# A selective scan's input products, two channel groups at a time, into a pair of PSUM banks of their own

## The chip, the cores and the metric

The kernel runs on one core of one Trainium2 chip. The metric is the device time of one execution in microseconds, the median of several runs. The profile is one further execution, recorded by the hardware profiler. The engines are called as the profile calls them: PE (matmul), PEld (its weight loads), DVE (the vector engine), ACT (the scalar engine, also called ScalarE), POOL (GpSimd) and SP, which here only issues DMAs.

## The reference, cut to what matters

A MetaFormer layer on four images of 256 channels and 32 x 32 points (1024 points), all in float32: a Mamba-like selective scan in four blocks of 64 channels, gated convolutions, attention with 8 heads, a depthwise convolution and projection, and then a mixture of 8 experts of which each point uses 2. The change is about the scan:

```python
def selective_scan(u, dt, Bm, Cm, A, Dp):          # u, dt: (B, 1024, 128); Bm, Cm: (B, 1024, 16); A: (128, 16)
    dA = jnp.exp(dt[..., None] * A)
    dBu = (dt * u)[..., None] * Bm[:, :, None, :]

    def step(h, inp):
        dA_t, dBu_t, C_t = inp
        h = dA_t * h + dBu_t
        return (h, jnp.einsum('bds,bs->bd', h, C_t))
    ...                                              # scan over the 1024 points
    return ys.transpose(1, 0, 2) + u * Dp
```

For each of 4 images and 4 blocks there are thus 128 channels x 16 states, each a recurrence over 1024 points. The products `dBu` are what the change touches.

## The kernel before, in words

**The scan.** The 1024 points are cut in two halves of 512, so there are 4 x 4 x 2 = 32 parts `(b, n, h)`. The 128 x 16 recurrences of a part do not fit the 128 partitions at once: they are done in `NSTEP` = 16 steps of 128 rows, where step `i = 4q + g` holds channel group `g` (32 channels) under four states of group `q`. Each step makes:

- `decay` (L718, ACT): `dA = exp(dt * A)`, three steps ahead (`LEAD` = 3);
- `inflow` (L728, DVE): `dBu = (dt * u) * B`, a 128x512 product, written to PSUM;
- `step` (L739, DVE): the recurrence itself, one scan operation over 512 points, which reads `dA` from SBUF and `dBu` from PSUM and writes `hs`; then (L747, POOL) `hs * C`, written over `dA`. In the first half the last column is kept by a small ACT copy (L745), and the second half starts from it;
- `sums_of` (L757, PE): adds the four states of each channel by a matmul with `quads`, into the bank `yp` of the part.

The inputs have to be laid out so that all four state rows carry the same channels. `spread_dt` (L681) copies one channel group of `dt` and `dt * u` by four DMAs on SP from the part's tile `dt` into a tile `dts` with 4 KB a partition; there are six such tiles (pool `steps4`). `spread_c` (L704) does the same for `C` from DRAM, and `spread_b` (L710) makes the rows of `B` by matmuls into a PSUM bank `bs`, one for each `q`.

**PSUM.** There are eight banks of 128 x 512 floats, all in one pool under one tag. Every matmul result draws one, and so does `dBu`, except that for `g` = 3 the product is written over `bs`, which is not read again afterwards. A bank is given out when all that used it has been done; the framework places the semaphore waits, between two operations of the same engine as well.

**The order.** All engines run the program in the order written. `scan(at, i, stop)` issues what belongs to one step: matmuls and DMAs for the next part by the tables `before`, `behind` and `group`, then `decay` for step i+3, then `inflow` for step i+1, then `step` for i. Background work (normalisations, convolutions, products around attention) consists of generators, and after each step `beat()` lets each of them issue a piece. For images 1 to 3 the scan stops in the middle of the image (`stop`), the attention of the image before runs with only light work beside it, and `resume` takes the scan up again when the last steps of attention have been issued.

**Attention.** `attention(b)` has 32 steps `(g, h, kt)`: `logits` makes four `st` banks by matmul (L1126), ACT takes their exponentials (L1136), and PE adds up values (L1175) and sums (L1147) in two further banks `av`, which live for the eight `kt` of a block and are read by `end_block` (L1159, L1163) in the second step of the next block.

**Experts.** After the scan PE works through tiles of 256 or 320 points (`Experts.tile`): a hidden layer (L2332, banks `h`), then the output `y` (L2365) into a bank of its own, which DVE reads with the bias (L2383, or L2374 and L2375 for a last block of 64 points). From the second tile on, the weights lie in the tiles of the scan's step sizes: three of `dts` and one of `dt` for each tile of points, so that two tiles' weights are there at a time.

Of the kernel before, what the change touches and what calls it, by code (L numbers as in the profile page):

```python
# [9 lines left out]
F32 = mybir.dt.float32  # L10
AF = mybir.ActivationFunctionType
ALU = mybir.AluOpType
AX = mybir.AxisListType

P = 128
C = 256
NC2 = C // P
HH = WW = 32
N = HH * WW
HALF = 512  # L20
NB, DM, DIN, DS, DTR, KC = 4, 64, 128, 16, 4, 4
NHEAD, HD = 8, 32
NE, DFF = 8, 1024
NHC = DFF // P
# [10 lines left out]
_AT = {}  # L35
# [43 lines left out]
def network(  # L79
# [27 lines left out]
    nc = tc.nc  # L107
    shifted = sums is None
    B = x.shape[0]

    cpool = ctx.enter_context(tc.tile_pool(name="consts", bufs=1))
    psum = ctx.enter_context(tc.tile_pool(name="psum", bufs=8, space=bass.MemoryType.PSUM))

    def ps_tile(name):

# [10 lines left out]
    def col(name, i=0, rows=slice(0, P)):  # L126
# [3 lines left out]
    ident = cpool.tile([P, P], F32, name="ident")  # L130
# [5 lines left out]
    eps5 = cpool.tile([P, 1], F32, name="eps5")  # L136
# [6 lines left out]
    nc.gpsimd.memset(one, 1.0)  # L143

    experts = Experts(
        ctx, tc, psum, B, vecs[:, _AT["b1"] : _AT["b1"] + NE * NHC], ident, eps5, ones_mean, Wg, bg,
        W1, W2, b2, out,
    )

# [1 line left out]
    with tc.tile_pool(name="w_conv", bufs=1) as wp, tc.tile_pool(  # L151
# [1 line left out]
    ) as act8, tc.tile_pool(name="act4", bufs=8) as act4, tc.tile_pool(  # L153
        name="act2", bufs=16
    ) as act2, tc.tile_pool(name="steps", bufs=2) as actd, tc.tile_pool(
        name="steps4", bufs=6
    ) as acts, tc.tile_pool(name="rows", bufs=3) as actc, tc.tile_pool(
        name="small", bufs=1
    ) as small, tc.tile_pool(
# [227 lines left out]
        def ps(name):  # L387

            return psum.tile([P, HALF], F32, tag="ps", name=name)
# [284 lines left out]
            )  # L674

        def spread_dt(b, n, h, g):
            t = T[b, n, h, "dts", g] = acts.tile(
                [P, 2, HALF], F32, tag="dts", name=f"dts_{b}_{n}_{h}_{g}"
            )
            for r in states:  # L680
                nc.sync.dma_start(t[r], T[b, n, h, "dt"][ts(g, 32)])  # L681

        def project_c(b, n):
            cp = T[b, n, "cp"] = ps(f"cp_{b}_{n}")
# [30 lines left out]
        def decay(b, n, h, i):  # L715
            q, g = divmod(i, GD)
            dA = T[b, n, h, "dA", i] = a2(f"dA_{b}_{n}_{h}_{i}")
            nc.scalar.activation(  # L718
                dA, T[b, n, h, "dts", g][:, 0, :], AF.Exp, scale=A[:, g, n, q : q + 1]
            )  # L720

        ends = []

        def inflow(b, n, h, i):
            q, g = divmod(i, GD)
            dBu = T[b, n, h, "bs", q] if g == GD - 1 else ps(f"dBu_{b}_{n}_{h}_{i}")
            T[b, n, h, "dBu", i] = dBu
            nc.vector.tensor_tensor(  # L728
                dBu, T[b, n, h, "dts", g][:, 1, :], T[b, n, h, "bs", q], ALU.mult
            )  # L730

        def step(b, n, h, i):
            q, g = divmod(i, GD)
            dBu = T.pop((b, n, h, "dBu", i))
            hs = a2(f"hs_{b}_{n}_{h}_{i}")
            if h == 0 and i == 0:
                T[b, n, "last"] = small.tile([P, NSTEP], F32, tag="last", name=f"last_{b}_{n}", bufs=2)
            last = T[b, n, "last"][:, i : i + 1]
            nc.vector.tensor_tensor_scan(  # L739
                hs, T[b, n, h, "dA", i], dBu, 0.0 if h == 0 else last, ALU.mult, ALU.add  # L740
            )
            if h == 0:
                ends.append((last, hs[:, HALF - 1 : HALF]))
            if ends and (h == 1 or len(ends) > 2):
                nc.scalar.copy(*ends.pop(0))  # L745
            dA = T[b, n, h, "dA", i]
            nc.gpsimd.tensor_tensor(dA, hs, T[b, n, h, "cs", q], ALU.mult)  # L747
# [92 lines left out]
        def scan(at, i, stop):  # L840

            b, n, h = parts[at]
            q, g = divmod(i, GD)
            if g == 1 and q + 1 < GS:
                spread_b(b, n, h, q + 1)
            if at > 0:
                for what, *args in before.get(i, ()):
                    if parts[at - 1] not in finished:
                        what(*parts[at - 1], *args)
            if at + 1 < len(parts):  # L850
                for what, *args in behind.get(i, ()):
                    if what is not spread_b or not stop:
                        what(*parts[at + 1], *args)
            nb, nn = (b, n + 1) if n + 1 < NB else (b + 1, 0)
            if nb < B:
                for what, *args in group[h].get(i, ()):
                    what(nb, nn, *args)
            if g == 0 and q + 1 < GS:
                spread_c(b, n, h, q + 1)
            if g == 1 and q > 0:  # L860
                sums_of(b, n, h, q - 1)
            ahead = i + LEAD
            if ahead < NSTEP:
                decay(b, n, h, ahead)
            elif at + 1 < len(parts) and not stop:
                decay(*parts[at + 1], ahead - NSTEP)
            if i + 1 < NSTEP:
                inflow(b, n, h, i + 1)
            elif at + 1 < len(parts) and not stop:
                inflow(*parts[at + 1], 0)  # L870
            step(b, n, h, i)

        finished = set()

# [232 lines left out]
        def attention(b):  # L1107
# [12 lines left out]
            def logits(g, h, kt):  # L1120

                q, k = qk[g][:, 0, :], qk[g][:, 1, :]
                sts = [ps(f"st_{b}_{g}_{h}_{kt}_{i}") for i in range(4)]
                for i in range(4):
                    r = ts(i, HD)
                    nc.tensor.matmul(  # L1126
                        sts[i], k[r, ts(kt, P)], q[r, half(h)], start=True, stop=not shifted
                    )
                    if shifted:
                        nc.tensor.matmul(  # L1130
                            sts[i], ones[HD * i : HD * i + 1, :],
                            rows[g][HD * i : HD * i + 1, half(h)], start=False, stop=True,
                        )
                es = [a2(f"e_{b}_{g}_{h}_{kt}_{i}") for i in range(4)]
                for i in range(4):
                    ins = nc.scalar.activation(es[i], sts[i], AF.Exp, scale=1.0 / HD**0.5)  # L1136
                T["exps"] = ins if b == B - 1 else None
                return es
# [26 lines left out]
            for at, (g, h, kt) in enumerate(steps):  # L1165
                es = ahead
                if pairs and (kt % 2 or at > len(steps) - 6):
                    sum_pair()
                if at + 1 < len(steps):
                    ahead = logits(*steps[at + 1])  # L1170
                if kt == 0:

                    accs = [ps(f"av_{b}_{g}_{h}_{w}") for w in range(2)]
                for i in range(4):
                    nc.tensor.matmul(  # L1175
                        accs[0][ts(i, HD)], v8[:, kt, ts(4 * g + i, HD)], es[i],
                        start=(kt == 0), stop=(kt == NK - 1),
                    )
                if kt % 2 == 0:
                    first = es  # L1180
                else:
                    for i in range(4):
                        nc.vector.tensor_tensor(first[i], first[i], es[i], ALU.add)  # L1183
                    pairs.append((kt, accs[1], first))
                    if ending:
                        end_block(*ending.pop())
                if kt == NK - 1:
                    ending.append((g, h, *accs))
                if at == len(steps) - 3:
                    T["attended", b] = True  # L1190
                yield 1
# [204 lines left out]
        def tiles():  # L1396
# [34 lines left out]
            def load(n):  # L1431
                s, i = order[n]
                if n == 0:
                    w1 = [a8("w1_0")[:, :, 0:DFF]]
                    w2 = [a8("w2_0").rearrange("p c (k x) -> p (c k) x", x=C)]
                else:
                    w = [
                        acts.tile([P, N], F32, tag="dts", name=f"w_{n}_{k}") for k in range(3)
                    ] + [actd.tile([P, N], F32, tag="dt", name=f"w_{n}_3")]
                    w1, w2 = w[0:2], [v.rearrange("p (k c) -> p k c", c=C) for v in w[2:4]]  # L1440
                b2_s = actc.tile([P, C], F32, tag="cs", name=f"b2_{n}") if n else a2("b2_0")[:, 0:C]
                got[n] = experts.load(s, i, tables[s], w1, w2, b2_s)

# [195 lines left out]
class Experts:  # L1639
# [16 lines left out]
    ROW = C + 4  # L1656
    XR = [P, NT, ROW]

    def __init__(self, ctx, tc, psum, B, b1, ident, eps5, ones_mean, Wg, bg, W1, W2, b2, out):
        nc = self.nc = tc.nc  # L1660
        self.tc, self.psum, self.b1, self.ident, self.eps5 = tc, psum, b1, ident, eps5
        self.W1, self.W2, self.b2, self.out = W1, W2, b2, out
        self.B = B
        T, NT = self.T, self.NT
# [653 lines left out]
    def tile(self, j, s, got, hs, ys, apart=False):  # L2318
# [39 lines left out]
            added.append(ins)  # L2358

        for t, n in blocks:  # L2360
            if t % 2 == 0 or apart:
                yp = psum.tile([P, HALF], F32, tag="ps", name=f"y_{j}_{t}")
            parts = P // n
            for k in range(NHC):
                nc.tensor.matmul(  # L2365
# [154 lines left out]
```

## Time and profile before

| | |
|---|---|
| median of 3 runs | 2168.41 us (2166.26 to 2169.15) |
| the profiled execution | 2167.03 us, its span 2165.3 us |
| PE busy | 1931.0 us (89% of the span) |
| DVE busy | 1540.5 us (71%), 2252 instructions |
| ACT busy | 1212.3 us (56%) |
| POOL busy | 1043.4 us (48%) |

The span falls into the scan with its three interruptions (52 to 1438 us) and the rest, in which PE works on the last image's attention and the experts. The page's slices (each 54 us; a digit is the busy share in tenths) show it:

```
PE   6778778999977999988779999669999989999996
DVE  4989999957998989698899888987265354321121
```

DVE stands at 8 or 9 in most of the first 26 slices and low in the last 13; PE is the other way round. How to read the other views: a group's line has the line of the program, engine, operation, output and inputs, count, busy time in us, the mean of one in ns, and behind the second bar the time that the engine stood idle ahead of such an operation, with what ended it. A line of the timeline has the start and the duration in us. A line of the waits says who waited for whom: us in total, how often, and the longest.

### The profile page before, as it was taken

The numbers are of one execution on the slowest core, as the hardware profiler recorded it, in microseconds if no ns is written. First come the engines' busy times: TensorE is split into PE (matmuls) and PEld (weight loads), VectorE is DVE, ScalarE is ACT, GpSimd is POOL, SyncE is SP. The second block draws the span as 40 slices with busy tenths as digits, with TensorE's granted clock in tenths as the row PEclk, the third lists the DMA queues.
The fourth block names the chain that finished last, engine by engine and source line by source line (L and its number), as shares of the span: only waits on it lengthen the run. The fifth ranks groups of instructions, "written<-read, shape, count | busy, mean of one in ns | idle before, by whom it ended". The sixth has DMA issues, their size and how long they took to land. (4 is left out here: it accounts for less than half of the span.)

```text
span 2165.3 us, 28187 instructions
## 1 busy us (share of the span) xinstructions
PE 1931.0 (89%) x8690; PEld 867.6 (40%) x8690; DVE 1540.5 (71%) x2252; ACT 1212.3 (56%) x2272; POOL 1043.4 (48%) x931
## 2 busy tenths in 40 slices
PE   6778778999977999988779999669999989999996
PEld 2113112322211332223123223216652668888885
DVE  4989999957998989698899888987265354321121
ACT  4665657668777677776466876615268423222221
POOL 0887887812787850476877016662021012522131
PEclk8888999999999999998999999989999999999998
DMA  3555544401444431153634203444230165777764
GB/s 105 148 157 130 124 118 103 101 28 57 103 116 117 104 75 40 25 141 92 176 87 105 83 6 94 109 164 135 84 99 23 47 198 161 242 229 188 213 184 131
DMA packets 157087, 251.40 MB, mean 116 GB/s; under 512 B 34740, under 2 KB 101332, under 8 KB 156664
## 3 DMA queue, kind: packets, MB, share of 16 engines
q1 hardware_dynamic: 136560, 223.47, 37.3%
q0 software_dynamic: 12720, 17.32, 4.1%
q10 hardware_dynamic: 7640, 8.65, 1.2%
q8 instruction: 72, 1.18, 0.2%
q14 instruction: 95, 0.78, 0.1%
HBM read 137.22 MB, written 36.62 MB: 80 GB/s over the span
## 5 line engine op out<-in xcount | busy, mean ns | idle before, releaser
L747 POOL TENSOR_TENSOR dA<-hs,cs 128x512 f32<-128x512 f32 x512 | 681.1, 1339 | 376.9 <-DVE hs L739 249.8
L718 ACT ACTIVATE dA<-dts,A 128x512 f32<-128x512 f32 x512 | 359.0, 718 | 161.4 <-DMA dts<-dt 76.9
L757 PE MATMUL yp<-dA,quads 128*32 128x512 f32 x1024 | 286.3, 640 | 89.3 <-POOL dA L747 76.6
L2350 POOL DMA_INDIRECT Y<-ys,dest x68 | 109.6, 1612 | 424.3 <-DVE ys L2343 417.3
L1136 ACT ACTIVATE e<-st 128x512 f32<-128x512 f32 x512 | 263.7, 606 | 89.4 <-PE st L1126 89.2
L2337 ACT ACTIVATE hs<-h,b 128x256 f32<-128x256 f32 (+1 forms) x256 | 110.6, 478 | 343.6 <-PE h L2332 256.7
L728 DVE TENSOR_TENSOR dBu<-dts,bs 128x512 f32<-128x512 f32 x384 | 259.6, 677 | 46.0 <-PE bs L710 10.8
L739 DVE TENSOR_TENSOR_SCAN hs<-dA,last,dBu 128x512 f32<-128x512 f32 x192 | 243.6, 1269 | 3.0 <-issue 2.1
L2365 PE MATMUL y<-w,hs 128*128 128x256 f32 (+1 forms) x1088 | 242.4, 382 | 0.0
L2332 PE MATMUL h<-xT,w 128*128 128x256 f32 (+1 forms) x1024 | 239.7, 390 | 0.8 <-DVE xT L2295 0.8
L739 DVE TENSOR_TENSOR_SCAN hs<-dA,dBu 128x512 f32<-128x512 f32 x192 | 231.6, 1206 | 0.7 <-PE var L438 0.7
L1183 DVE TENSOR_TENSOR e<-e,e 128x512 f32<-128x512 f32 x256 | 168.2, 718 | 77.8 <-ACT e L1136 47.8
L2332 PEld LDWEIGHTS h<-xT,w 128*128 128x128 f32 x1024 | 195.2, 192 | 41.7 <-issue 8.0
L2365 PEld LDWEIGHTS y<-w,hs 128*128 128x128 f32 (+1 forms) x1088 | 197.3, 188 | 36.1 <-issue 9.0
L2295 DVE COPY xT<-xp 128x512 f32<-128x512 f32 (+1 forms) x36 | 23.3, 646 | 249.4 <-PE xp L2291 249.1
L710 PE MATMUL bs<-u,xpwT_s 128*32 128x512 f32 x1024 | 162.9, 669 | 40.3 <-DVE hs L739 17.3
L1126 PE MATMUL st<-qk 32*128 32x512 f32 x1024 | 174.0, 638 | 0.3
L757 PEld LDWEIGHTS yp<-dA,quads 128*32 128x32 f32 x1024 | 51.3, 114 | 303.4 <-POOL dA L747 198.7
L1175 PE MATMUL av<-e,v 128*32 128x512 f32 x1024 | 139.5, 604 | 0.0
L1953 POOL DMA_INDIRECT XS<-XR,to x64 | 65.4, 1022 | 92.0 <-ACT e L1136 53.9
L1126 PEld LDWEIGHTS st<-qk 32*128 32x128 f32 x1024 | 59.5, 183 | 115.3 <-issue 85.6
L1147 PE MATMUL av<-e,every 128*32 128x512 f32 x512 | 85.2, 596 | 2.7 <-DVE e L1183 2.6
(357 smaller groups left out, 2640.5 us busy)
## 6 DMA issues: line engine op xcount, KB each, us to landing
dts<-dt SPq DMA_DIRECT2D x512, 128.0 KB
w<-in_W_dram SPq DMA_DIRECT2D x124, 512.0 KB
cs<-cd SPq DMA_DIRECT2D x512, 64.0 KB
xs<-XS SPq DMA_DIRECT2D x32, 260.0 KB
xd<-xn SPq DMA_DIRECT2D x64, 128.0 KB
xn<-in_x_dram SPq DMA_DIRECT2D x8, 512.0 KB
XL<-xl SPq DMA_DIRECT2D x8, 512.0 KB
xl<-XL SPq DMA_DIRECT2D x4, 1024.0 KB
```

Of the source, the lines that this page charges most:

```text
L710: nc.tensor.matmul(bs[r], xpwT_s[:, n, s : s + 1].to_broadcast([P, 32]), T[b, n, "u"][:, half(h)], start=True, stop=True,)
L718: nc.scalar.activation(dA, T[b, n, h, "dts", g][:, 0, :], AF.Exp, scale=A[:, g, n, q : q + 1])
L728: nc.vector.tensor_tensor(dBu, T[b, n, h, "dts", g][:, 1, :], T[b, n, h, "bs", q], ALU.mult)
L739: nc.vector.tensor_tensor_scan(hs, T[b, n, h, "dA", i], dBu, 0.0 if h == 0 else last, ALU.mult, ALU.add)
L747: nc.gpsimd.tensor_tensor(dA, hs, T[b, n, h, "cs", q], ALU.mult)
L757: nc.tensor.matmul(T[b, n, h, "yp"][ts(g, 32)], quads, T[b, n, h, "dA", q * GD + g], start=False, stop=(q == GS - 1),)
L1126: nc.tensor.matmul(sts[i], k[r, ts(kt, P)], q[r, half(h)], start=True, stop=not shifted)
L1136: ins = nc.scalar.activation(es[i], sts[i], AF.Exp, scale=1.0 / HD**0.5)
L1175: nc.tensor.matmul(accs[0][ts(i, HD)], v8[:, kt, ts(4 * g + i, HD)], es[i], start=(kt == 0), stop=(kt == NK - 1),)
L1183: nc.vector.tensor_tensor(first[i], first[i], es[i], ALU.add)
L2332: nc.tensor.matmul(hp[:, i, :], w1(c, k0 + i), xT[:, c, :], start=(c == 0), stop=(c == NC2 - 1))
L2365: nc.tensor.matmul(yp[ts(k % parts, n), ts(t % 2, C)], hidden(k)[:, ds(t * P, n)], w2(k), start=(k < parts), stop=(k >= NHC - parts),)
```

## The change

`inflow` is done for two channel groups in one operation. A pool `psum_wide` of one tile with two neighbouring banks is added, and the common pool has six banks. `dBu` of two steps is one 128 x 2 x 512 operation into that pair, with `bs` repeated by a zero stride; the case `g` = 3 that wrote over `bs` is gone. The step sizes of two groups lie in one tile of 8 KB a partition, three tiles in place of six, and the DMAs are the same in number and size. In `scan` the product comes after `step`, at odd steps only, since there is one pair and the odd step's scan reads its second half. Outside the scan the pair of banks is used too: in attention with h = 0 for the two accumulators, with h = 1 for two of the four logits of some steps; in the experts for `y`. The experts' weights take the new tiles: one or two pairs by turns, with two `dt` tiles in the even ones.

```diff
-    psum = ctx.enter_context(tc.tile_pool(name="psum", bufs=8, space=bass.MemoryType.PSUM))
+    psum = ctx.enter_context(tc.tile_pool(name="psum", bufs=6, space=bass.MemoryType.PSUM))
+    wide_psum = ctx.enter_context(
+        tc.tile_pool(name="psum_wide", bufs=1, space=bass.MemoryType.PSUM)
+    )
+
+    def two_banks(name):
+
+        t = wide_psum.tile([P, 2, HALF], F32, tag="two", name=name)
+        return t
...
-        name="steps4", bufs=6
+        name="steps4", bufs=3
...
         def spread_dt(b, n, h, g):
-            t = T[b, n, h, "dts", g] = acts.tile(
-                [P, 2, HALF], F32, tag="dts", name=f"dts_{b}_{n}_{h}_{g}"
-            )
+            k, at = divmod(g, 2)
+            if at == 0:
+                T[b, n, h, "dts", k] = acts.tile(
+                    [P, 2, 2, HALF], F32, tag="dts", name=f"dts_{b}_{n}_{h}_{k}"
+                )
+            t = T[b, n, h, "dts", k]
             for r in states:
-                nc.sync.dma_start(t[r], T[b, n, h, "dt"][ts(g, 32)])
+                nc.sync.dma_start(t[r, at], T[b, n, h, "dt"][ts(g, 32)])
...
         def inflow(b, n, h, i):
             q, g = divmod(i, GD)
-            dBu = T[b, n, h, "bs", q] if g == GD - 1 else ps(f"dBu_{b}_{n}_{h}_{i}")
-            T[b, n, h, "dBu", i] = dBu
+            dBu = two_banks(f"dBu_{b}_{n}_{h}_{i}")
             nc.vector.tensor_tensor(
-                dBu, T[b, n, h, "dts", g][:, 1, :], T[b, n, h, "bs", q], ALU.mult
-            )
+                dBu, T[b, n, h, "dts", g // 2][:, :, 1, :],
+                T[b, n, h, "bs", q].rearrange("p (a t) -> p a t", a=1)
+                .to_broadcast([P, 2, HALF]), ALU.mult,
+            )
+            for k in range(2):
+                T[b, n, h, "dBu", i + k] = dBu[:, k, :]
...
-            if i + 1 < NSTEP:
+            step(b, n, h, i)
+            if i % 2 and i + 1 < NSTEP:
                 inflow(b, n, h, i + 1)
-            elif at + 1 < len(parts) and not stop:
+            elif i % 2 and at + 1 < len(parts) and not stop:
                 inflow(*parts[at + 1], 0)
-            step(b, n, h, i)
...
-                sts = [ps(f"st_{b}_{g}_{h}_{kt}_{i}") for i in range(4)]
+                sts = []
+                if h and 3 <= kt < NK - 2 * g:
+                    both = two_banks(f"st_{b}_{g}_{h}_{kt}")
+                    sts = [both[:, i, :] for i in range(2)]
+                sts += [ps(f"st_{b}_{g}_{h}_{kt}_{i}") for i in range(len(sts), 4)]
...
-                    accs = [ps(f"av_{b}_{g}_{h}_{w}") for w in range(2)]
+                    if h:
+                        accs = [ps(f"av_{b}_{g}_{h}_{w}") for w in range(2)]
+                    else:
+                        both = two_banks(f"av_{b}_{g}_{h}")
+                        accs = [both[:, w, :] for w in range(2)]
...
-                    w = [
-                        acts.tile([P, N], F32, tag="dts", name=f"w_{n}_{k}") for k in range(3)
-                    ] + [actd.tile([P, N], F32, tag="dt", name=f"w_{n}_3")]
-                    w1, w2 = w[0:2], [v.rearrange("p (k c) -> p k c", c=C) for v in w[2:4]]
+                    def pair(k):
+                        t = acts.tile([P, 2, N], F32, tag="dts", name=f"w_{n}_{k}")
+                        return [t[:, i, :] for i in range(2)]
+
+                    w1 = pair(0)
+                    w2 = pair(1) if n % 2 else [
+                        actd.tile([P, N], F32, tag="dt", name=f"w_{n}_{k}") for k in (2, 3)
+                    ]
+                    w2 = [v.rearrange("p (k c) -> p k c", c=C) for v in w2]
...
         for t, n in blocks:
-            if t % 2 == 0 or apart:
-                yp = psum.tile([P, HALF], F32, tag="ps", name=f"y_{j}_{t}")
+            if t == 0:
+                both = self.two_banks(f"y_{j}")
+            yp = both[:, t if apart else t // 2, :]
```

## The prediction

> **What bounds the kernel now.** I read the page's slices and groups first, then the stretches, then the timeline of DVE inside one part, then the waits of DVE and SP. Two stretches, the first of nothing but scan, the second of attention with the scan stopped (columns: length, then busy us of PE, PEld, DVE, ACT, POOL):
>
> ```profile
> 200.00:300.00 100.00, 79.26 (x286) 16.42 (x278) 100.00 (x115) 60.91 (x113) 84.64 (x70) 0.98 0.53 128
> 428.00:530.00 102.00, 101.60 (x644) 29.31 (x643) 66.53 (x86) 75.25 (x146) 20.68 (x15) 1.00 0.14 42
> ```
>
> DVE is the bound in the scan: 100 of 100 us. POOL follows with 85. In attention it is PE. The page's groups of the scan:
>
> ```profile
> L747 POOL TENSOR_TENSOR dA<-hs,cs 128x512 f32<-128x512 f32 x512 | 681.1, 1339 | 376.9 <-DVE hs L739 249.8
> L728 DVE TENSOR_TENSOR dBu<-dts,bs 128x512 f32<-128x512 f32 x384 | 259.6, 677 | 46.0 <-PE bs L710 10.8
> L739 DVE TENSOR_TENSOR_SCAN hs<-dA,last,dBu 128x512 f32<-128x512 f32 x192 | 243.6, 1269 | 3.0 <-issue 2.1
> ```
>
> POOL waits for DVE's hs, and the scan operation itself hardly waits. Adding up the time from each scan operation to the next, without the three gaps of over 90 us in which attention runs, gives 1095.6 us, of which DVE was idle only 76. So nearly every microsecond of DVE in these 1096 us is paid at the end. What one step costs is seen in the timeline (start, duration):
>
> ```profile
> 246.21 0.67 DVE L728 TENSOR_TENSOR dBu<-dts,bs 128x512 f32<-128x512 f32 x1
> 246.79 1.20 DVE L739 TENSOR_TENSOR_SCAN hs<-dA,bs 128x512 f32<-128x512 f32 x1
> 247.92 0.67 DVE L728 TENSOR_TENSOR dBu<-dts,bs 128x512 f32<-128x512 f32 x1
> 248.50 1.20 DVE L739 TENSOR_TENSOR_SCAN hs<-dA,dBu 128x512 f32<-128x512 f32 x1
> 249.62 0.67 DVE L728 TENSOR_TENSOR dBu<-dts,bs 128x512 f32<-128x512 f32 x1
> ```
>
> The recorded durations overlap: the product takes 0.58 us from start to start, not 0.67, the scan 1.13, not 1.20. A step is 1.705 us (1.77 in the second half of a sequence, whose scan takes 1269 ns). Each operation starts about 0.08 to 0.09 before the one ahead of it ends. That works because neighbours are independent: the product of step i+1 stands between the product and the scan of step i. Where an operation needs its direct predecessor on DVE, the trace shows something else:
>
> ```profile
> 23.86 0.69 DVE L513 TENSOR_TENSOR xl<-xn,r 128x512 f32<-128x512 f32 x1
> 24.58 0.69 DVE L514 TENSOR_TENSOR xn<-xn,r 128x512 f32<-128x512 f32 x1
> 25.31 0.55 DVE L515 TENSOR_SCALAR xn<-xn,V 128x512 f32<-128x512 f32 x1
> ...
> 1909.98 0.42 DVE L2374 TENSOR_TENSOR other<-other,b 64x256 f32<-64x256 f32 x1 [1.62 <-ACT other L2373]
> 1910.50 0.42 DVE L2375 TENSOR_TENSOR ys<-y,other 64x256 f32<-64x256 f32 x1
> ```
>
> L514 overwrites what L513 reads (write after read), L515 reads what L514 wrote: both start 0.03 to 0.04 us after the end. L2375 reads what L2374 wrote and waits for PE besides, so that its wait on DVE sits in a semaphore instruction of its own ahead of it: 0.10 after the end. So a dependence on the direct predecessor costs 0.12 or 0.19 us against the overlap.
>
> **What the skill says.** The Trainium skill, "Vector Engine (DVE) Microarchitecture Reference", 5.2 Measured stream behaviour on trn2, gives 1.0417 ns per column plus about 75 ns per instruction after overlap. The trace agrees roughly: 0.58 is 533 ns of columns plus 50. Joining two products can then save some 0.05 us, not the 0.14 that the recorded durations suggest. "VectorE: DVE Perf Modes", The DRAIN you can't avoid, says that a read after a write on this engine needs a semaphore, and that the semaphore costs nothing extra. The first part is what the waits in the trace look like; the second this trace contradicts by the 0.12 to 0.19 above, and the trace is used.
>
> **The change, part by part.**
>
> *One product in place of two.* 256 products of 128x1024 in place of 512 of 128x512. The nearest row is the 128x1024 f32 multiply of L1252:
>
> ```profile
> L1252 DVE TENSOR_TENSOR xc<-xc,r_lgn 128x1024 f32<-128x1024 f32 x8 | 9.5, 1201 | 0.0
> ```
>
> I take 1.205 (0.672 plus 512 columns at 1.0417 ns). Upper bound 1.35 (the fixed part paid once per bank, +37 us over 256), lower 1.11 (columns and the 0.045 seen between starts, -24 us). Recorded busy time falls by 256 x (2 x 0.675 - 1.205) = 37 us, which will look like a gain.
>
> *The order and the single pair of banks.* There is one pair tile, so the product of the next pair can only follow the odd step's scan, which has just read it, and the even step's scan follows the product that it reads. Both are now dependences on the direct predecessor. The scan's wait comes with that for dA from ACT, so I take 0.10; the product's is alone in half the cases (0.035) and beside bs from PE in the other half (0.10), so 0.07. One pair then takes 0.07 + 1.205 + 0.10 + 1.205 - 0.08 + 1.205 = 3.705 us against 2 x 1.705 = 3.41: **0.295 us more**. Where background work of DVE stands between, the scan's wait is hidden; I counted such work there in 46 of 252 pairs, and these cost 0.295 - 0.19 = 0.105. So 210 x 0.295 + 46 x 0.105 = 67 us. Some of today's products already pay a wait for their bank's last scan, and the mean overlaps are 0.066 and 0.086 rather than 0.08 and 0.09: some 9 us, leaving **+58**. Bounds of the waits: both 0.035 gives +0.19 per pair before, some +34 after these deductions; both 0.10 or a little above gives +66. Behind the waiting product are the scan, then POOL's multiply and PE's sums, all with slack against DVE.
>
> *Bank waits that go.* Products no longer draw from the common banks. Of the 46 us idle before L728 these are waits for a bank that ACT still read:
>
> ```profile
> DVE dBu L728 <- PE bs L710: 10.8, 8, 5.3
> DVE dBu L728 <- ACT e L1136: 6.2, 3, 3.1
> DVE dBu L728 <- ACT g L944: 5.9, 3, 5.4
> DVE dBu L728 <- ACT qk L1101: 4.5, 3, 1.5
> DVE dBu L728 <- ACT xr L1356: 4.1, 2, 3.0
> ```
>
> With smaller ones about 26 us, and the product also comes up to 1.13 us later relative to its inputs. What is late next is ACT itself, whose dA the same step needs: I credit **-15** (0 to -30). Other idle time of DVE in the scan absorbs some: **-6** (0 to -20). For the rest the banks balance: today's scan holds about two product banks besides bs and yp, and two banks are taken from eight.
>
> *Step sizes in pair tiles.* Same DMAs, same bytes. The third group's transfer now waits for the release of a whole pair, which comes a scan and half a product later (2.4 us). It already waits:
>
> ```profile
> SPq L681 <- DVE dBu L728: 114.5, 29, 9.0
> ```
>
> From that release to landing of the fourth group I read 233.0 to 242.96 at one boundary: 9.9 us, with the cs copies between them on SP. The pair's product needs it about 10 us after the release. So it falls about level: today's margins run from 0.4 to 2.7 us and shrink by about 1.4. A few of 31 boundaries stall about 1 us: **+5** (0 to +30). DVE would stall, then POOL and PE.
>
> *Attention.* With h=0 the two accumulators lie in the pair and six banks carry st, as before. With h=1 the pair carries two st and is reused only when both are read; four other banks remain. The fourth st of a step has to wait for the same exponential as before, so steady state is level; the last two steps of g=1 have four banks, not six, and the first bs shares them: **+2** (-8 to +8).
>
> *Experts.* y has one pair; its reader L2383 takes 689 ns, and the next y comes a whole hidden layer later (32 tiles in some 600 us of the tail, about half of each hidden layer: an estimated 5 us or more). Weights keep two tiles in flight. 0 (0 to +5), covered by that distance; without it, 0.7 us for each of 32 tiles.
>
> Sum: 58 - 15 - 6 + 5 + 2 = **+44 us** on the profiled execution's 2167.0 (span 2165.3), so 2211; the median of the runs, 2168.4, is 1.4 above that execution. I say 2211.
>
> **Rivals.** (A) The products' saving arrives: if the two dependences were hidden (or the release needed no wait), a pair would be 1.205 + 2.41 - 0.25 = 3.365, 0.045 less, with the 9 us above 0.08 less: -20 us, and with the bank waits gone -26 more: about 2122. For it: fewer instructions, DVE the bound, and 46 us idle before L728. Against: every adjacent dependence that I found in the trace has its gap. (B) The step sizes land late at nearly every boundary: 31 x 1 more, about 2240. For: 114.5 us of waits on this very release and a margin of 0.4 us in the first part. Against: the margins elsewhere. (C) DVE's idle 76 us soak up the waits: 2168 to 2180. Against: the idle time lies in some 49 steps, the extra in all.
>
> **Chances.** Main case 0.70, B 0.12, C 0.09, A 0.09. A difference of 0.2% (4 us) is what a measurement of this kernel can tell: faster 0.10 (A and the edge of C), same 0.03, slower 0.87. The range takes the wait bounds (+34 to +66), the credits and B: 2175 to 2246.
>
> **What would show it.** Right: L728 with 256 operations near 1.2 us; DVE's recorded busy time 37 us lower while the scan's stretches are longer; in the timeline gaps of 0.03 to 0.10 us before and after each product, pairs of 3.6 to 3.7 us. Wrong: starts before the predecessor's end at both places (A); waits of L728 for dts of over 20 us (B); an operation above 1.3 us, or attention longer by over 5 us each.

## The result: 4.4% slower, and the profile after

The changed kernel takes 2263.7 us (median of 6 runs, 2260.8 to 2267.4) against 2168.8: ratio 1.0443, 95% interval 1.0427 to 1.0458. The profiled execution has a span of 2261.5 us against 2165.3, 96 us more. The direction was forecast, the size (44 us) was not. The stretches that answer to the two shown of before, the first all scan, the second the first image's attention:

```profile
219.00:319.00 100.00, 76.95 (x250) 14.88 (x249) 94.88 (x79) 53.84 (x101) 76.05 (x64) 0.98 0.48 116
455.00:567.00 112.00, 104.25 (x645) 29.09 (x647) 63.55 (x84) 76.69 (x147) 17.43 (x14) 0.95 0.12 37
```

In the scan DVE is busy for 94.9 of 100 us where it was 100, and it does fewer operations: time has gone into gaps on the engine that bounds the stretch. In attention PE is busy 93% of the stretch where it was 99.6%, and its granted clock (the third number from the end) is 0.95, not 1.00. The page's groups of the scan (L739 is now the product, L754 the scan operation, L762 POOL's multiply):

```profile
L762 POOL TENSOR_TENSOR dA<-hs,cs 128x512 f32<-128x512 f32 x512 | 664.0, 1312 | 460.1 <-DVE hs L754 311.5
L739 DVE TENSOR_TENSOR dBu<-dts,bs 128x1024 f32<-128x1024 f32 x256 | 314.6, 1229 | 38.7 <-PE bs L721 16.0
L754 DVE TENSOR_TENSOR_SCAN hs<-dA,last,dBu 128x512 f32<-128x512 f32 x256 | 315.6, 1267 | 27.3 <-PE yp L772 8.6
L754 DVE TENSOR_TENSOR_SCAN hs<-dA,dBu 128x512 f32<-128x512 f32 x256 | 300.2, 1207 | 19.5 <-PE var L446 4.9
```

The product is one of 256 and takes 1229 ns; 314.6 us against 345.7 (the 512 products of before): 31 us less busy. The idle time ahead of it went from 46.7 to 38.7 us, but ahead of the scan operation from 5 to 47. POOL, which was not the bound, just waits longer. In the timeline of DVE (start, duration, and a count where operations are merged):

```profile
252.37 1.23 DVE L739 TENSOR_TENSOR dBu<-dts,bs 128x1024 f32<-128x1024 f32 x1
253.73 2.33 DVE L754 TENSOR_TENSOR_SCAN hs<-dA,dBu 128x512 f32<-128x512 f32 x2
256.09 1.23 DVE L739 TENSOR_TENSOR dBu<-dts,bs 128x1024 f32<-128x1024 f32 x1
257.45 2.33 DVE L754 TENSOR_TENSOR_SCAN hs<-dA,dBu 128x512 f32<-128x512 f32 x2
259.82 1.23 DVE L739 TENSOR_TENSOR dBu<-dts,bs 128x1024 f32<-128x1024 f32 x1
```

The product ends at 253.60 and its scan starts at 253.73, 0.13 later; the second scan ends at 256.06 and the next product starts at 256.09, 0.03 later. A pair takes 3.72 us, where two steps took 3.41.

Where the 96 us lie, from the start times in both traces: the scan without its three interruptions 1095.6 to 1147.5 us (**+52**); the four attentions, each from its first to its last exponential, 375.4 to 416.4 (**+41**); the rest about +3, with some 5 us more behind the last exponential, in the tail with the experts, and some 2 less elsewhere.

Attention is where the forecast had next to nothing (+2). The longest waits of PE for another engine there, from the list of waits (total, count, longest):

```profile
PE st L1145 <- DVE qk L1182: 24.4, 8, 3.3
PE st L1145 <- ACT e L1155: 4.3, 12, 0.7
```

Eight waits, seven of 3.3 us and one of 1.4: two per attention, one for each block with h = 1. L1182 is the last operation of `end_block`. One of them in the timeline of the last image's attention, with some operations left out:

```profile
1697.39 1.14 PE L1145 MATMUL st<-qk 32*128 32x512 f32 x8
...
1698.46 1.06 PE L1198 MATMUL av<-e,v 128*32 128x512 f32 x8
1698.55 2.06 ACT L1155 ACTIVATE e<-st 128x512 f32<-128x512 f32 x4 [1.07 <-PE st L1145]
...
1700.48 0.71 ACT L1174 ACTIVATE low<-av,added 128x512 f32<-128x512 f32 x1
1701.22 0.63 ACT L1179 ACTIVATE low<-low 128x512 f32<-128x512 f32 x1
...
1701.97 0.69 DVE L1182 TENSOR_TENSOR qk<-av,low 128x512 f32<-128x512 f32 x1
...
1702.81 2.09 PE L1145 MATMUL st<-qk 32*128 32x512 f32 x8 [3.28 <-DVE qk L1182]
...
1704.83 1.94 PE L1198 MATMUL av<-e,v 128*32 128x512 f32 x8
1704.92 2.06 ACT L1155 ACTIVATE e<-st 128x512 f32<-128x512 f32 x4 [2.98 <-PE st L1145]
```

And the same place before the change:

```profile
1619.71 1.84 PE L1126 MATMUL st<-qk 32*128 32x512 f32 x8
1620.72 0.71 ACT L1155 ACTIVATE low<-av,added 128x512 f32<-128x512 f32 x1
...
1622.22 0.69 DVE L1163 TENSOR_TENSOR qk<-av,low 128x512 f32<-128x512 f32 x1
```

Before, the logits of the fourth step (1619.71) ran ahead of `end_block`'s last read of the accumulators (1622.22). After, the first two of them lie in the pair that these accumulators still hold, so PE stands still for 3.28 us until DVE has multiplied, and ACT, which has nothing to read, stands still for 2.98 us. The wait costs a second time: the eight matmuls of st then take 2.09 us and those of av 1.94, where one step earlier they took 1.14 and 1.06. In stretches of about 2 us (the granted clock is the third number from the end):

```profile
1697.00:1699.40 2.40, 2.40 (x24) 0.47 (x16) 2.18 (x4) 1.33 (x3) 0.00 (x0) 1.00 0.16 55
1702.80:1704.80 2.00, 1.99 (x8) 0.53 (x8) 0.00 (x0) 0.00 (x0) 0.00 (x0) 0.50 0.03 8
1704.80:1706.50 1.70, 1.70 (x12) 0.40 (x12) 0.00 (x0) 1.57 (x4) 0.00 (x0) 0.50 0.00 0
1706.50:1708.40 1.90, 1.90 (x12) 0.20 (x4) 1.56 (x3) 0.49 (x2) 0.00 (x0) 0.50 0.00 0
1708.40:1710.50 2.10, 2.10 (x20) 0.53 (x16) 0.94 (x2) 0.86 (x2) 0.00 (x0) 0.96 0.00 0
```

After the standstill TensorE was granted half its clock for 5.6 us. All seven waits of 3.3 us have such a stretch at half clock in or just behind them, the one of 1.4 us has none. In this block the interval between the exponentials of the third and fourth steps grew from 3.3 to 6.4 us, and the next from 2.4 to 4.7.

### The profile page after: what moved, and what is told of

The parts are those of the page before. It is cut to its first block, busy times and chain, and to the rows that moved or that the text cites. A ratio compares the mean times of both kernels' runs of the same rounds, so it can differ in the third digit from the quotient of the medians.

```text
span 2261.5 us, 27679 instructions
## 1 busy us (share of the span) xinstructions
PE 1995.1 (88%) x8690; PEld 877.2 (39%) x8690; DVE 1564.0 (69%) x1996; ACT 1212.5 (54%) x2272; POOL 1021.0 (45%) x931
## 5 line engine op out<-in xcount | busy, mean ns | idle before, releaser
L762 POOL TENSOR_TENSOR dA<-hs,cs 128x512 f32<-128x512 f32 x512 | 664.0, 1312 | 460.1 <-DVE hs L754 311.5
L772 PE MATMUL yp<-dA,quads 128*32 128x512 f32 x1024 | 316.4, 649 | 108.5 <-POOL dA L762 84.9
L739 DVE TENSOR_TENSOR dBu<-dts,bs 128x1024 f32<-128x1024 f32 x256 | 314.6, 1229 | 38.7 <-PE bs L721 16.0
L754 DVE TENSOR_TENSOR_SCAN hs<-dA,last,dBu 128x512 f32<-128x512 f32 x256 | 315.6, 1267 | 27.3 <-PE yp L772 8.6
L754 DVE TENSOR_TENSOR_SCAN hs<-dA,dBu 128x512 f32<-128x512 f32 x256 | 300.2, 1207 | 19.5 <-PE var L446 4.9
L1145 PE MATMUL st<-qk 32*128 32x512 f32 x1024 | 186.2, 664 | 28.6 <-DVE qk L1182 24.4
L1166 PE MATMUL av<-e,every 128*32 128x512 f32 x512 | 80.1, 629 | 0.7 <-DVE e L1206 0.7
```

What stands on the lines that cost most here:

```text
L739: nc.vector.tensor_tensor(dBu, T[b, n, h, "dts", g // 2][:, :, 1, :], T[b, n, h, "bs", q].rearrange("p (a t) -> p a t", a=1) .to_broadcast ...
L754: nc.vector.tensor_tensor_scan(hs, T[b, n, h, "dA", i], dBu, 0.0 if h == 0 else last, ALU.mult, ALU.add)
L772: nc.tensor.matmul(T[b, n, h, "yp"][ts(g, 32)], quads, T[b, n, h, "dA", q * GD + g], start=False, stop=(q == GS - 1),)
L1145: nc.tensor.matmul(sts[i], k[r, ts(kt, P)], q[r, half(h)], start=True, stop=not shifted)
```

## The experiments

The ratios are to the kernel before on the same chip, with their 95% intervals. Times of stages are from one profiled execution each.

**order_only: the order of before and after, in the kernel before.**

```diff
+            step(b, n, h, i)
             if i + 1 < NSTEP:
                 inflow(b, n, h, i + 1)
             elif at + 1 < len(parts) and not stop:
                 inflow(*parts[at + 1], 0)
-            step(b, n, h, i)
```

> The kernel before, with step issued ahead of inflow in every step and nothing else: eight banks, single products of 128x512, six dts tiles. Each scan now follows directly on DVE the product that it reads. Theory 1 (a dependence on the direct predecessor is what the scan's part of the loss is made of): in the changed kernel such a scan started 0.13 us after its product's end, before it started 0.088 us ahead of it, so 0.22 us for each step without background work of DVE between (about 428 of 512): some +94 us, about 2262, the range 2240 to 2280, with the product's own start still ahead of the scan's end, and attention unchanged. Theory 2 (the order costs nothing, the wide operation or the pair of banks does): 2169, plus or minus 6.

Measured: 2243.8 us, ratio 1.0349 (1.0323 to 1.0375). The timeline of DVE:

```profile
254.21 0.68 DVE L728 TENSOR_TENSOR bs<-dts,bs 128x512 f32<-128x512 f32 x1
255.01 1.28 DVE L739 TENSOR_TENSOR_SCAN hs<-dA,last,bs 128x512 f32<-128x512 f32 x1
256.21 0.68 DVE L728 TENSOR_TENSOR dBu<-dts,bs 128x512 f32<-128x512 f32 x1
```

The scan starts 0.12 us after its product's end (254.89), the product still 0.08 ahead of the scan's end. Over the 428 scans that directly follow their product the mean gap (gaps of over 0.2 us left out) is +0.12 us, where it was -0.086: 89 us. The scan's stage grew by 84 us (1179.6), attention not at all (375.5). So a change of order alone, with the same operations, costs 3.5%. It came in at the low end of what was expected: idle gaps of over 0.2 us on DVE fell from 71 to 47 us, presumably since a later product finds its bank and its inputs ready. The 84 us are not these two alone: DVE's operations in the stage are recorded 29 us longer in sum, 5 of them the scans' and most of the others the background work's, and the products start a little earlier against the scans ahead of them. Why the operations are longer is not shown. Theory 2 is out.

**one_bank: both dependences at every step.** The order of order_only, and in `inflow` (with a seventh and an eighth bank divided accordingly):

```diff
-            dBu = T[b, n, h, "bs", q] if g == GD - 1 else ps(f"dBu_{b}_{n}_{h}_{i}")
+            dBu = own_bank(f"dBu_{b}_{n}_{h}_{i}")
```

> The kernel before with the same order as order_only, and all products in one bank of their own (seven common banks; attention takes that bank for its fourth logit, but not in the last two steps). Every product now overwrites what the scan just ahead of it has read, and every scan reads the product just ahead: both dependences of the changed kernel, but at every step, not at every second one. Theory 1: per step 0.22 us as in order_only and 0.05 instead of -0.08 ahead of the product, 0.13 more: about 428 x 0.35 + 84 x 0.13 = 161, less 9 that some products pay today, some +150 us, about 2320 (2290 to 2350), about three times the scan's part of the change. Theory 2: as order_only, 2169 to 2180.

Measured: 2328.1 us, ratio 1.0741 (1.0713 to 1.0769).

```profile
264.09 0.69 DVE L736 TENSOR_TENSOR dBu<-dts,bs 128x512 f32<-128x512 f32 x1
264.92 1.28 DVE L747 TENSOR_TENSOR_SCAN hs<-dA,last,dBu 128x512 f32<-128x512 f32 x1
266.29 0.70 DVE L736 TENSOR_TENSOR dBu<-dts,bs 128x512 f32<-128x512 f32 x1
```

Now both starts come after the predecessor's end: means, again without the gaps of over 0.2 us, of +0.13 (428 scans after their product) and +0.04 us (508 products after a scan, -0.08 in order_only). The scan's stage grew by 127 us, 43 more than in order_only. That is the price of the write after read, about 0.12 us for each product less some idle time that it absorbs. The total was as expected, but not its make-up: 50 us of it are attention (425.2). I take the reason to be that the fourth logit's only bank has to be read before the next fourth logit: in the last image's first block with h = 1 the last four steps take 2.4, 3.8, 2.1 and 4.1 us, where before they took 2.1, 3.1, 2.1 and 3.1. So a single buffer in attention would cost there too, without any accumulator in it; no run tests this by itself.

**att_last: the pair for the last two logits.**

```diff
-                sts = []
-                if h and 3 <= kt < NK - 2 * g:
+                pair = h and 3 <= kt < NK - 2 * g
+                sts = [ps(f"st_{b}_{g}_{h}_{kt}_{i}") for i in range(2 if pair else 4)]
+                if pair:
                     both = two_banks(f"st_{b}_{g}_{h}_{kt}")
-                    sts = [both[:, i, :] for i in range(2)]
-                sts += [ps(f"st_{b}_{g}_{h}_{kt}_{i}") for i in range(len(sts), 4)]
+                    sts += [both[:, i, :] for i in range(2)]
```

> The changed kernel, but in attention the pair of banks holds the last two of the four logits of a step, not the first two. Theory 1 (PE is in order, and the first logits of the fourth step of a block with h=1 wait in the pair for end_block of the block before, with the other two stuck behind them): the first two now go ahead and feed ACT while the others wait, the interval from the third to the fourth step's exponentials falls from 6.4 us towards 3.3 to 4.5, and 15 to 35 of the 41 us that the four attentions lost come back: 2228 to 2248. Theory 2 (attention is slower because six banks are too few or because of the granted TensorE clock, 0.936 against 0.961): 2264, plus or minus 6.

Measured: 2259.7 us, ratio 1.0421 (1.0389 to 1.0453); attention 410.9. The expectation failed, and the total lies where theory 2 had it. The first interval did fall, from 6.4 to 3.3 us, but the wait only moved. PE still waits eight times for `end_block`:

```profile
PE st L1145 <- DVE qk L1182: 15.7, 8, 2.2
```

The last two logits of that step come late: the following interval is 5.0 us in the block quoted above and 6.7 in the other one of that image, and the later ones alternate between 2.1 and 4.1 where they had been 2.3 and 2.9. As I read it, with the pair behind, every step ends on a buffer that the step before has only just given up. In that block this run has no stretch at half clock, so that there the waits alone make it longer.

**att_pair_st: the accumulators out of the pair.**

```diff
-                if h and 3 <= kt < NK - 2 * g:
+                if kt < NK - 2 * (g and h):
...
-                    if h:
-                        accs = [ps(f"av_{b}_{g}_{h}_{w}") for w in range(2)]
-                    else:
-                        both = two_banks(f"av_{b}_{g}_{h}")
-                        accs = [both[:, w, :] for w in range(2)]
+                    accs = [ps(f"av_{b}_{g}_{h}_{w}") for w in range(2)]
```

> The changed kernel, but attention's accumulators always lie in common banks and the pair always holds the first two logits, so that end_block never holds the pair. Theory 1: the long intervals at the third and fourth steps go, since the pair is free as soon as two exponentials have been taken; two common banks are left for the other two logits while two blocks' accumulators live, and attention comes back to within 2 us each of the kernel before: 2222 to 2235. Theory 2 (six banks are too few, or the clock): 2264, plus or minus 6.

Measured: 2239.5 us, ratio 1.0331 (1.0304 to 1.0358); attention 385.5. The same place in the timeline:

```profile
1678.31 1.61 PE L1145 MATMUL st<-qk 32*128 32x512 f32 x8 [0.17 <-ACT e L1155]
...
1680.59 0.69 DVE L1182 TENSOR_TENSOR qk<-av,low 128x512 f32<-128x512 f32 x1
```

The fourth step's logits run ahead of `end_block` again. With the same six and two banks, and again the first two logits in the pair, now in nearly every step, 31 of the 41 us are back; what remains is 2 to 4 us for each attention. The total is some 4 us above what was expected. (The profiled execution, from which 385.5 is, took 2233.1 us, the shortest of the four.) Too few banks as such (theory 2) can account for the remaining 10 us at most.

**att_from4: the pair one step later.** In the changed kernel:

```diff
-                if h and 3 <= kt < NK - 2 * g:
+                if h and 4 <= kt < NK - 2 * g:
```

> The changed kernel, with the pair used for logits from the fifth step of a block with h=1 on (kt of 4), not from the fourth (kt of 3). If the wait is for end_block of the block before, the fourth step now goes ahead with four common banks and the interval before it falls from 6.4 to about 3.3 us; the fifth step may wait in its place if end_block is still later. I expect half of the 41 us of the four attentions back: their sum 390 to 402 against 416.4 in the changed kernel and 375.4 before, and about 2240 to 2252 in all. If the cause is another, 416 and 2264.

Measured, one execution: 2233.1 us, attention 388.0. One character of the source gives back 28 of the 41 us, more than expected: by the fifth step `end_block` is through, and the interval there is 2.7 us (before: 2.7), not 4.6, in the third image's first such block. PE no longer waits for `end_block` there, and none of the four attentions has a stretch at half clock. This fixes the cause of these 28 us: the handover of the pair from the accumulators to the logits, one step too early. The other 13 us lie in other steps, where the changed kernel has most of them too: over the four images some 7 in the first steps of the blocks with h = 0 and some 5 in the last two steps of an attention. No run shows what makes these.

**dts_only: the step sizes in pair tiles, in the kernel before.**

```diff
-        name="steps4", bufs=6
+        name="steps4", bufs=3
...
-                nc.sync.dma_start(t[r], T[b, n, h, "dt"][ts(g, 32)])
+                nc.sync.dma_start(t[r, at], T[b, n, h, "dt"][ts(g, 32)])
```

> The kernel before with the step sizes of two groups in one tile (three tiles of 8 KB a partition for six of 4 KB) and the experts' weights placed accordingly; products, order, banks and attention as before. Theory 1 (the pair tiles are nearly free): a later release of the first pair stalls DVE at few part boundaries, 0 to +5 us, 2168 to 2175. Theory 2 (the prediction's rival B): the third and fourth group's transfers land late at nearly every boundary, DVE waits for dts 20 to 30 us more, 2190 to 2200.

Measured: 2176.3 us, ratio 1.0046 (1.0030 to 1.0061), about 10 us (6 to 13). The scan's stage grew by 7.1 us, DVE's gaps of over 0.2 us by 6.7. So the pair tiles are not free, and rival B's 20 to 30 us are not there either. Waits for dts went from 7.7 to 11 us; the rest is spread over waits for ACT and POOL that I can't tie to one transfer.

**y_common: the experts' output out of the pair.** att_pair_st, and in `Experts.tile`:

```diff
-            if t == 0:
-                both = self.two_banks(f"y_{j}")
-            yp = both[:, t if apart else t // 2, :]
+            if t % 2 == 0 or apart:
+                yp = psum.tile([P, HALF], F32, tag="ps", name=f"y_{j}_{t}")
```

> att_pair_st with the experts' output y back in common banks as before, the rest as there. Theory 1 (y's single pair makes PE wait for DVE's reading of the tile before, which is what the tail after the scan lost beside attention): the time from the first tile's hidden layer to the last's falls by about 5 us of the 680 in att_pair_st, 2230 to 2236. Theory 2 (y costs nothing, the tail's loss is another's): 680, and 2239 plus or minus 4.

Measured: 2225.7 us, ratio 1.0262 (1.0237 to 1.0288). That is 4 us below what was expected. From the first tile's hidden layer to the last's it takes 671.5 us, not 680.5 (669.6 in the kernel before); 2.4 us of that are attention's. From the last exponential to the end it takes 487.9 us, not 495.0 (488.0 before). The changed kernel's own list of waits has waits of this kind, though only 3.1 us of them:

```profile
PE y L2395 <- DVE ys L2413: 3.1, 4, 0.8
```

This is the best version with a pair that I ran, and it is still 2.6% slower than the kernel before. What it keeps is the scan's 54 us (1149.8). None of the runs points to a version that beats the kernel before. The product in pairs without the dependences, which needs two pairs of banks, wasn't tried. An estimate from the measured numbers: two products take 2 x 0.675 - 0.15 of overlap, a joined one 1.229 - 0.08, which saves some 0.05 us a pair or 13 us, with four banks bound for it.

## Why the prediction was right in its direction and wrong in its size

**The bound and the pair of operations: right.** The pair was put at 3.705 us and takes 3.72. The product was put at 1.205 and takes 1.229 (it saves 31 us of busy time, not 37). The gaps between products and scans, overlaps counted as negative, went from -70 us to +20 over all direct neighbours: +90, against 95 in the working (58 and the 37 of busy time). order_only shows the first dependence by itself, one_bank what the second adds.

**Bank waits that go: over-credited.** The sum had -15 and -6. DVE's gaps of over 0.2 us in the scan went from 70.7 to 63.6, so -7 in all, the pair tiles of the step sizes included. The product waits less, as argued, but what is late next is the scan operation: its idle time went from 5 to 47 us, of which only some 25 are the new gap. The working named ACT's dA as the next to be late; PE's yp and var stand ahead of it in the group lines. The term was -21 and should have been about -14, with the step sizes' +7 beside it (put at +5), if the 6.7 us of gaps in dts_only hold in the changed kernel too. The scan's sum is -31 + 90 - 7 = 52, as measured; it was forecast as 42.

**Attention: the step that failed.** The prediction gave it +2 (-8 to +8) with the words "With h=1 the pair carries two st and is reused only when both are read ... The fourth st of a step has to wait for the same exponential as before, so steady state is level". That compares logits with logits. It leaves out the first use of the pair in a block, when it is not logits that hold it but the accumulators of the block with h = 0, until `end_block`'s last multiply on DVE. That this read comes late was in the code (`end_block` is issued in the second step, after the third step's logits), and what is queued behind the wait, which the prediction says for the product, was not asked here: PE runs in the order written, so the other two logits, av and the sums stood behind. It measured +41. The intervals in which PE stands grew by 22 us over the four images (the waits are 24.4 us on PE), those right after them, mostly at half clock, by 12.5, and later ones gave 4.6 back: 30, and att_from4 returns 28. The other 11 to 13 us have another cause, which is open.

**Experts: put at 0 (0 to +5).** From the last exponential to the end the changed kernel takes 492.9 us, not 488.0: +5, the edge of the range. The hidden layer covers most, not all, of DVE's read; y_common shows it.

**The range** was too narrow by this one term: with +41 for attention the same sum gives 2250, with the scan at 52 as well 2260, and with the rest's 3 it gives 2263. Rival A (the saving arrives) is out by the 0.13 us in the timeline, rival B by dts_only, rival C by the gaps that are there and not absorbed.

## What to carry to other kernels

Before joining two operations, write down who is whose direct predecessor on the engine, before and after. DVE overlapped independent neighbours by 0.08 us here, and lost 0.21 us at each new read after write (order_only) and 0.12 at each new write after read (one_bank), two to four times the 0.05 us that a joined product is estimated to save. When a buffer changes from several to one, list every user of it over time, above all the handover from one kind of user to another; a level steady state says nothing about it. And look for what stands behind a wait on PE: a standstill of 3 us was paid once as a wait and once more as a halved clock.

## What I had not expected of the hardware

The clock: around a standstill of 3.28 us TensorE was granted 0.50 in the midst of a stretch at 1.00, 5.6 us of it after the standstill, which nearly doubled the matmuls (st 1.14 to 2.09 us). The Trainium skill, "TensorE: Matmul & The Clock Gate", Part 1: The HAM clock gate (the "warmup" mystery), puts the fall to half rate after at least one idle window of about 3.4 us. The traces agree with the length of the window, but it need not be idle. All stretches at half clock begin on one grid of 3.41 us in each trace. Cut on this grid, from 20 us on, the changed kernel's trace has 42 windows at full clock that a window at half clock followed: in 41 of them PE was busy for at most 48% of the window. In the 528 that full clock followed, it was busy for at least 42%, and so it is in all nine traces; windows before half clock that were busy for over half occur, up to five in a trace. The windows before the half clock at the seven waits of 3.3 us were busy for 11 to 44%; the window with the wait of 1.4 us was busy for 60%. In att_pair_st a wait of 1.70 us and the start of a second one left PE busy for 37% of one window, and half clock followed. So by these traces it is not the length of a single wait that counts, but whether PE is busy for somewhat under half of such a window.

The wait on the own engine: where the product's only wait is in the instruction itself, it started 0.034 us after its predecessor's end (the median of 193 in the changed kernel). Where one semaphore instruction stands ahead and the two hold two waits, the gap was 0.10 us (40 products and 26 scans), and with three waits 0.13 (170 scans). What sets the gap is not shown: in one_bank 89 products with two semaphore instructions and five waits started after 0.034 us all the same.
